# Outgoing transfers placed one iteration later on the transfer queue, and each state's row of C fetched by one transfer instead of two

## The chip, the cores and the metric

The kernel runs on one core of a Trainium2 chip. The metric is the device time of one execution in microseconds. A core has five engines that each work through their own list of instructions in order: TensorE (PE in the profile, with its weight loads as PEld), VectorE (DVE), ScalarE (ACT), GpSimd (POOL) and SyncE (SP). In this kernel every transfer between on-chip memory (SBUF) and device memory (HBM) is issued by SP. SP waits in order: a transfer whose data are not ready holds up every transfer behind it. The bytes are moved by 16 DMA engines of the core.

## The reference

The input is 8 images of 64 x 64 tokens with 96 channels. Layer 0 is a two-dimensional state-space block, layer 1 an attention without softmax followed by a quantized feed-forward layer. What matters here is the state-space part:

```python
xs = jnp.stack([s0, s1, s0[..., ::-1], s1[..., ::-1]], axis=1)       # 4 directions of 4096 tokens, 192 channels
x_dbl = jnp.einsum('bkdl,kcd->bkcl', xs, x_proj_weight)
dts, Bs, Cs = jnp.split(x_dbl, [DT_RANK, DT_RANK + D_STATE], axis=2) # 6, 16, 16 rows
delta = jax.nn.softplus(jnp.einsum('bkrl,kdr->bkdl', dts, dt_projs_weight) + dt_projs_bias[None, :, :, None])
def step(hst, inp):                                                 # h has 192 x 16 states for each image and direction
    u_t, d_t, B_t, C_t = inp
    hst = hst * jnp.exp(d_t[..., None] * A) + (d_t * u_t)[..., None] * B_t[:, :, None, :]
    return (hst, jnp.einsum('bkdn,bkn->bkd', hst, C_t))
```

Every one of the 16 states n has its own row C[n] over the tokens, and the state of every channel is multiplied by that same row.

## The kernel before

**The scan.** A step m is one image, one pair of directions (q = 0 forward, q = 1 backward) and one chunk of T = 512 tokens; there are 8 x 2 x 8 = 128 steps. The 128 partitions hold two directions of 64 channels each, and G = 3 groups make up the 192 channels. The main loop at the end of `run` has one iteration for each step and state: 128 x 16 = 2048 iterations. In iteration i, ScalarE makes the decays for state i + 2 (`decay`, L966) and on some states the products with B (`times_b`, L988), VectorE scans state i (`recur`, L1009), TensorE brings the products of state i + 1 into PSUM (`turn`, L996) and adds up state i - 4 (`reduce`, L1044), and GpSimd multiplies state i - 1 by its row of C (`read`, L1030).

**The rows of C.** `prologue` computes the projected rows of a step, writes the 32 rows of C (2 directions x 16 states) to a buffer `crow` in HBM (L910), and `fetch` reads them back, one state at a time, copied to 64 partitions for each direction (L957):

```python
cc = made[m].c[n] = pool.tile([P, T], F32, tag="cc", name=f"cc_{i}", bufs=5)
for d in range(2):
    nc.sync.dma_start(
        out=cc[d * GC : (d + 1) * GC], in_=made[m].crow[d * NS + n : d * NS + n + 1, :].to_broadcast([GC, T])
    )
```

`fetch(i + 4)` is the last thing of iteration i. There are five `cc` buffers, so it takes the buffer that `read(i - 1)` of the same iteration has just used, and SP waits for GpSimd there.

**The work beside the scan.** While one image is scanned, the next image's front (normalization, convolution, the walk along the diagonals: `front`) and the last image's tail (join of the four directions, attention, feed-forward: `tail`) run in the gaps. They are Python generators that a planner, the class `Work`, advances. A generator yields the engine that its next piece needs ("A", "V", "G", "P"), its estimated time and how many iterations it has to lie back; `LAGS` has the defaults, and `proceed` keeps the iteration from which the piece may be placed. `next` opens an iteration and places the pieces with the tag "S"; `at("A")`, `at("V")` and so on are called at fixed places of the iteration. `finish` runs iterations without the scan until a condition holds; it is called at the seventh iteration of every image, to see that the streams of work of the image before have ended.

**The outgoing transfers.** A generator issues a transfer out of SBUF directly behind the instruction that makes its data, in the same piece. So the transfer stands on SP's list ahead of the `fetch` of that iteration. These are the gate and the convolved image (`convolve`, L561 and L568), the walked sequence (`walk`, L599), the middle result and the transposed tokens (`join`, L689 and L728), the output (`layers`, L834), the rows of C (`prologue`, L910), and a step's sums (`place`, L1072, and `spread`, L1089). Some of what comes in matters as well: `join` loads its tiles `y` at L634 into buffers that L728 has read from two or three chunks before.

Of the kernel before, what the change touches and what calls it, by code (L numbers as in the profile page):

```python
# [254 lines left out]
    return "P", us, lag, "long" if long else "short"  # L255


SPIN = ("P", 0.0, -1, False)


class Work:
# [104 lines left out]
    def finish(self, enough):  # L366

        self.alone = True
        while not enough():
            self.next()  # L370
            for tag, place in (("A", 0), ("V", 0), ("P", 2), ("G", 0)):
                self.at(tag, place)
        self.alone = False
        self.credit = dict.fromkeys(self.PLACES, 0.0)

    def hurry(self, enough):

        self.alone = self.hurried = True
        while not enough():
            self.now += 1  # L380
            for tag, place in (("A", 0), ("V", 0), ("P", 2), ("G", 0)):
                self.at(tag, place)
        self.alone = self.hurried = False

# [89 lines left out]
def front(tc, work, x, k, at, b):  # L474
# [8 lines left out]
    with tc.tile_pool(name=f"f1_{b}", bufs=1, **area) as p1, tc.tile_pool(name=f"f2_{b}", bufs=2, **area) as p2:  # L483
        flat = p1.tile([DM + 1, WP * WP + 4], F32, tag="xp", name="xp")
        xp = flat[:, 0 : WP * WP].rearrange("p (h w) -> p h w", w=WP)

        def clear():
            yield gp(4.0)

            nc.gpsimd.memset(flat[0:DM, 0 : WP + 1], 0.0)  # L490
            nc.gpsimd.memset(flat[0:DM, WP * (WP - 1) - 1 :], 0.0)
            nc.gpsimd.memset(flat[0:DM, 2 * WP - 1 : 2 * WP - 1 + HH * WP].rearrange("p (h w) -> p h w", w=WP)[:, :, 0:2], 0.0)
            nc.gpsimd.memset(flat[DM : DM + 1], 1.0)
            while not at.measured:
                yield SPIN

        yield [clear()], 1

        normed = set()

        def norm(c):

            xt = fetched(nc, p2, x, b, c, 3)
            ps = yield bank(0.45, 4)
            v = channels(nc, k, ps, xt)
            yield act(0.65)
            nc.scalar.activation(
                xp[0:DM, 1 + 8 * c : 9 + 8 * c, 1 : WW + 1], v.rearrange("p (h w) -> p h w", w=WW),
                AF.Identity, scale=at.norm[:, 0:1], bias=at.norm[:, 1:2],
            )  # L510
            work.release(ps)
            normed.add(c)

        TILES = HH * WP // P
        groups = [range(4 * c, min(4 * c + 4, TILES) if c < NCH - 1 else TILES) for c in range(NCH)]

        def convolve(c):

            pre = p2.tile([P, 5, DI], F32, tag="pre", name="pre")
            z = p2.tile([HC, 2, CH], F32, tag="z", name="z")  # L520
            while not all(r in normed for r in range(min(c + 2, NCH))):
                yield SPIN
            left = [0]

            def out(ps, to, v):
                left[0] += 1
                yield dve(0.6, 1)
                nc.vector.tensor_copy(to, v)
                work.release(ps)
                left[0] -= 1  # L530

            tiles = groups[c]
            for first in range(0, len(tiles), 2):
                some = tiles[first : first + 2]
                ps = yield bank(0.33, 0, True)
                v = view(ps, P, len(some), DI)
                for j, t in enumerate(some):
                    for i in range(9):
                        if i or j:
                            yield pe(0.33)  # L540
                        o = t * P + i // 3 * WP + i % 3
                        nc.tensor.matmul(  # L542
                            v[:, j, :], flat[:, o : o + P], k.wf[:, i, :], start=(i == 0), stop=(i == 8), skip_group_check=True
                        )
                work.full(ps)
                work.start(out(ps, pre[:, first : first + len(some), :], v))
            for a in range(2):
                ps = yield bank(0.85, 0)
                nc.tensor.matmul(
                    view(ps, HC, CH // WW, WW), k.w_in[:, DI + a * HC : DI + (a + 1) * HC],  # L550
                    xp[0:DM, 1 + 8 * c : 9 + 8 * c, 1 : WW + 1], start=True, stop=True,
                )
                work.start(out(ps, z[:, a, :], view(ps, HC, CH)))
            yield pe(0.0, 1)
            while left[0]:
                yield SPIN
            yield act(4.5)
            nc.scalar.activation(pre[:, 0 : len(tiles), :], pre[:, 0 : len(tiles), :], AF.Silu)
            nc.scalar.activation(z, z, AF.Silu)
            k.tables()  # L560
            nc.sync.dma_start(out=at.gate[:, :, c * CH : (c + 1) * CH], in_=z)  # L561

            image = at.image[0 : HH * DOUBLE].rearrange("(h a x c) -> h x a c", a=2, c=DI, x=WW)
            for j, t in enumerate(tiles):
                for h in range(t * P // WP, min((t * P + P - 1) // WP + 1, HH)):
                    lo, hi = max(t * P, h * WP), min(t * P + P, h * WP + WW)
                    if lo < hi:
                        nc.sync.dma_start(  # L568
                            out=image[h, lo - h * WP : hi - h * WP],
                            in_=pre[lo - t * P : hi - t * P, j, :].unsqueeze(1).to_broadcast([hi - lo, 2, DI]),  # L570
                        )

        ahead = [norm(c) for c in range(3)]
        yield ahead + [j(c + 3 * (j is norm)) for c in range(NCH) for j in (convolve, norm) if j is convolve or c + 3 < NCH], 4

    with tc.tile_pool(name=f"f3_{b}", bufs=3, **area) as p2:

        def walk(c):
# [12 lines left out]
            for g in range(G):  # L591
                ps = yield bank(0.45, 4 if g == 0 else 0)
                for i in range(TB):
                    nc.tensor.transpose(ps[:, i * P : (i + 1) * P], ut[:, i, g].rearrange("p d i -> p (d i)"), k.ident)
                yield act(0.6)
                nc.scalar.copy(u[:, g, :], ps)
                work.release(ps)
            for d in range(2):
                nc.sync.dma_start(  # L599
                    out=at.seq[d][:, c * T : (c + 1) * T].rearrange("(g i) t -> i g t", i=GC),  # L600
                    in_=u[d * GC : (d + 1) * GC],
                )
# [5 lines left out]
def tail(tc, work, x, out, k, at, b, last=False):  # L608
# [4 lines left out]
    with tc.tile_pool(name=f"t1_{b}", bufs=1, **area) as p1:  # L613
# [5 lines left out]
        with tc.tile_pool(name=f"t2_{b}", bufs=8 if last else 2, **area) as p2:  # L619
# [3 lines left out]
            def join(c):  # L623
# [61 lines left out]
                        )  # L685
                yield act(0.5)
                nc.scalar.copy(t, po)
                if not last:
                    nc.sync.dma_start(out=at.mid[:, s, :], in_=t)  # L689
                work.release(ps)  # L690
                yield dve(1.7)
                for i in range(4):
# [32 lines left out]
                if last:  # L725
                    kept[c] = t, xaT
                else:
                    nc.sync.dma_start(out=at.turned[:, c * CH : (c + 1) * CH], in_=xaT)  # L728
                joined.add(c)

# [31 lines left out]
        with tc.tile_pool(name=f"t3_{b}", bufs=8 if last else 3, **area) as p2:  # L762

            def layers(c):
# [66 lines left out]
                yield gp(2.0)  # L831
                nc.gpsimd.tensor_tensor(y16, y16, k.b2q, ALU.add)
                nc.gpsimd.tensor_tensor(t, t, y16, ALU.add)
                nc.sync.dma_start(out=out[b].rearrange("(t p) c -> p t c", p=P)[:, s, :], in_=t)  # L834

            yield [layers(c) for c in range(NCH)], 8 if last else 3
# [2 lines left out]
def run(tc, psum, dram, x, out, w, NB):  # L839
# [39 lines left out]
    def prologue(m):  # L879
# [26 lines left out]
        x = o.x = tile("x", [NX, T])  # L906
        nc.scalar.activation(x, v, AF.Identity, bias=w.xb)  # L907
        work.release(ps)
        o.crow = dram.tile([2 * NS, T], F32, tag="crow", name=f"crow_{m}", bufs=3)
        nc.sync.dma_start(out=o.crow, in_=x[XC:NX, :])  # L910


        delta = tile("delta", [P, G, T])
        for g in range(G):
            ps = yield bank(0.85)
            nc.tensor.matmul(ps, w.ws[:, q, g, :], x[0 : 2 * NR + 1, :], start=True, stop=True)  # L916
            yield dve(0.6)
            nc.vector.tensor_copy(delta[:, g, :], ps)  # L918
            work.release(ps)
# [32 lines left out]
    def fetch(i):  # L952

        m, n = divmod(i, NS)
        cc = made[m].c[n] = pool.tile([P, T], F32, tag="cc", name=f"cc_{i}", bufs=5)
        for d in range(2):
            nc.sync.dma_start(  # L957
                out=cc[d * GC : (d + 1) * GC], in_=made[m].crow[d * NS + n : d * NS + n + 1, :].to_broadcast([GC, T])
            )

    def decay(i):
        m, n = divmod(i, NS)
# [95 lines left out]
    def place(m):  # L1058
# [7 lines left out]
        for d in range(2):  # L1066
# [1 line left out]
                rows[:, d].rearrange("p k (g i) -> p k g i", i=GC),  # L1068
                y.rearrange("p (k g) (d i) -> p d k g i", g=G, d=2)[:, d],
            )  # L1070
        if q == 0:
            nc.sync.dma_start(out=image(b).part[:, c, :], in_=ys)  # L1072
        else:
            work.start(spread(m, rows), urgent=True)

    def spread(m, rows):
        b, q, c = steps[m]
        for d in range(2):
            yield gp(1.8, 1)
            nc.gpsimd.tensor_tensor(  # L1080
                rows[:, d], rows[:, d], other[m].rearrange("p (d k c) -> p d k c", d=2, k=TB)[:, d], ALU.add
            )
            stride = (3 * WW + 1) * DI if d == 0 else (3 * WW - 1) * DI
            for v in range(2):
                for again in range(2):
# [194 lines left out]
```

## Time and profile before

| what | value |
|---|---|
| time, median of 3 runs | 11243.42 us (11231.5 to 11244.23) |
| the profiled execution's own time | 11245.66 us |
| its span, first to last instruction | 11243.9 us |
| PE, DVE, ACT, POOL busy | 81%, 84%, 84%, 83% of the span |
| PE weight loads busy | 68% of the span |
| L1030 on POOL (state times C) | 2048 x 3457 ns = 7079.9 us |
| L1009 on DVE (the scan) | 5376 x 1262 ns and 768 x 1201 ns |
| DMA packets | 1122742, 1206.98 MB, 107 GB/s on average |
| share of the 16 DMA engines' time | 40.3% |
| mean granted TensorE clock | 0.907 |

All four computing engines are busy for more than four fifths of the span, none of them all the time. The table's busy times are of one profiled execution. "Share of the DMA engines' time" is the time that all packets took, over 16 times the span. In the profile "SPq" is SP as the issuer of transfers, and a line such as "DMA cc<-crow" is a transfer between its issue and its landing.

### The profile page before, as it was taken

How to read it: one execution, taken by the hardware profiler on the slowest of the kernel's cores; microseconds unless marked ns; L12 is line 12 of the kernel's file. 1: busy time of each engine (PE TensorE's matmuls, PEld its weight loads, DVE VectorE, ACT ScalarE, POOL GpSimd, SP SyncE). 2: the span in 40 equal slices, each digit the busy share in tenths (PEclk: the TensorE clock that was granted, in tenths of full speed). 3: DMA queues.
4: the chain of work that ended last, by engine and by line, in shares of the span. 5: the costliest groups of instructions: out<-in, count | busy, mean ns of one | idle time of the engine just before them, and what ended most of it. 6: DMA issues, size and time to landing. Idle time of an engine off the chain costs nothing.

```text
span 11243.9 us, 182845 instructions
## 1 busy us (share of the span) xinstructions
PE 9140.0 (81%) x60885; PEld 7661.4 (68%) x60885; DVE 9396.9 (84%) x10582; ACT 9455.9 (84%) x19651; POOL 9365.4 (83%) x7047
## 2 busy tenths in 40 slices
PE   6888788878888788878888788887888878878884
PEld 5677677666676667766677666776667666666663
DVE  2988988888888888888888888888898888989993
ACT  3888888888888888888888888888898888888883
POOL 1877987899878998789987899779997799998994
PEclk8999999888998889988999898998999988889886
DMA  3335333543335443354334543345433543432332
GB/s 91 106 92 143 100 98 92 144 118 102 97 93 149 110 108 95 96 144 113 102 92 113 138 107 102 92 118 134 109 99 90 133 119 104 108 103 84 99 94 63
DMA packets 1122742, 1206.98 MB, mean 107 GB/s; under 512 B 452790, under 2 KB 730007, under 8 KB 1121799
## 3 DMA queue, kind: packets, MB, share of 16 engines
q1 hardware_dynamic: 1121798, 1195.28, 40.3%
q8 instruction: 485, 7.95, 0.3%
q14 instruction: 459, 3.75, 0.1%
HBM read 874.83 MB, written 319.98 MB: 106 GB/s over the span
## 4 chain that ended last, share of the span: by engine, by line
PE 24%; ACT 23%; DVE 17%; POOL 14%; issue 10%; DMA 7%; SPq 4%; DVEq 0%; POOLq 0%; ACTq 0%
DVE h L1009 11%; ACT feedT L988 9%; POOL h L1030 8%; ACT decay L966 7%; PE y L1044 7%; PE feed L996 7%; DMA cc<-crow 4%; DVE feed L1013 4%; PE bank L542 3%; SPq L587 2%; PE bank L894 2%; PE feed L998 1%; ACT L63 1%; POOL du L928 1%; DMA y<-wide 1%
## 5 line engine op out<-in xcount | busy, mean ns | idle before, releaser
L1030 POOL TENSOR_TENSOR h<-h,cc 128x1536 f32<-128x1536 f32 x2048 | 7079.9, 3457 | 458.3 <-DMA cc<-crow 228.9
L1009 DVE TENSOR_TENSOR_SCAN h<-decay,carry,feed 128x512 f32<-128x512 f32 x5376 | 6514.2, 1262 | 810.2 <-PE feed L996 704.8
L966 ACT ACTIVATE decay<-delta,a_neg 128x512 f32<-128x512 f32 x6144 | 3975.0, 714 | 1116.4 <-DVE h L1009 1114.4
L996 PE MATMUL feed<-ident,feedT 128*128 128x128 f32 x16896 | 3090.8, 303 | 1649.1 <-DVE h L1009 1084.6
L1044 PE MATMUL y<-ident,h 128*128 128x128 f32 x24576 | 3847.4, 290 | 130.7 <-POOL h L1030 47.4
L996 PEld LDWEIGHTS feed<-ident,feedT 128*128 128x128 f32 x16896 | 2209.1, 155 | 2246.9 <-ACT feedT L988 840.8
L988 ACT ACTIVATE feedT<-duT,rows 128x192 f32<-128x192 f32 x10240 | 3673.7, 445 | 17.6 <-PE feed L996 14.7
L1044 PEld LDWEIGHTS y<-ident,h 128*128 128x128 f32 x24576 | 3164.5, 152 | 525.2 <-issue 410.3
L1013 DVE TENSOR_TENSOR feed<-feed,du 128x512 f32<-128x512 f32 x1920 | 1200.4, 685 | 162.2 <-PE feed L998 146.5
L1025 POOL COPY carry<-h 128x3 f32<-128x3 f32 x2048 | 402.5, 197 | 877.0 <-DVE h L1009 803.2
L1009 DVE TENSOR_TENSOR_SCAN h<-decay,feed 128x512 f32<-128x512 f32 x768 | 879.5, 1201 | 118.9 <-PE feed L996 106.8
L542 PE MATMUL bank<-wf,xp 97*128 97x192 f32 x4266 | 851.9, 332 | 0.0
L998 PE MATMUL feed<-x,pick 77*128 77x512 f32 x1280 | 708.8, 636 | 3.9
L542 PEld LDWEIGHTS bank<-wf,xp 97*128 97x128 f32 x4266 | 692.8, 194 | 5.4 <-issue 4.6
L928 POOL TENSOR_TENSOR du<-delta,u 128x1536 f32<-128x1536 f32 x128 | 448.4, 3503 | 188.8 <-ACT delta L921 188.8
L916 PE MATMUL bank<-x,ws 13*128 13x512 f32 x764 | 435.5, 650 | 5.6 <-ACT x L907 5.6
L979 POOL TENSOR_TENSOR feedT<-duT,rows 128x512 f32<-128x512 f32 x384 | 396.2, 1060 | 4.7 <-PE feed L996 4.7
L894 PE MATMUL bank<-wx,u 128*128 128x77 f32 x3048 | 360.0, 275 | 0.0
L894 PEld LDWEIGHTS bank<-wx,u 128*128 128x128 f32 x3048 | 352.3, 193 | 1.9 <-ACT duT L936 0.2
L918 DVE COPY delta<-bank 128x512 f32<-128x512 f32 x382 | 256.7, 672 | 86.5 <-PE bank L916 86.1
L934 PE MATMUL bank<-ident,du 128*128 128x128 f32 x1532 | 251.8, 291 | 65.1 <-POOL du L928 61.8
L998 PEld LDWEIGHTS feed<-x,pick 77*128 77x128 f32 x1280 | 211.5, 200 | 97.6 <-DVE h L1009 44.8
(261 smaller groups left out, 6957.4 us busy)
## 6 DMA issues: line engine op xcount, KB each, us to landing
cc<-crow SPq DMA_DIRECT2D x4096, 128.0 KB
u<-seq SPq DMA_DIRECT2D x256, 384.0 KB
wide<-ys SPq DMA_DIRECT2D x512, 192.0 KB
ut<-image SPq DMA_DIRECT2D x768, 64.0 KB
seq<-us SPq DMA_DIRECT2D x128, 384.0 KB
part<-ys SPq DMA_DIRECT2D x64, 768.0 KB
y<-part SPq DMA_DIRECT2D x64, 768.0 KB
y<-wide SPq DMA_DIRECT2D x256, 192.0 KB
```

The costliest lines, as they stand in the source:

```text
L542: nc.tensor.matmul(v[:, j, :], flat[:, o : o + P], k.wf[:, i, :], start=(i == 0), stop=(i == 8), skip_group_check=True)
L894: nc.tensor.matmul(v[:, j, :], u[:, g, j * P : (j + 1) * P], w.wx[:, q, g, :], start=(g == 0), stop=(g == G - 1))
L916: nc.tensor.matmul(ps, w.ws[:, q, g, :], x[0 : 2 * NR + 1, :], start=True, stop=True)
L928: nc.gpsimd.tensor_tensor(du, delta, u, ALU.mult)
L966: nc.scalar.activation(decays[i][:, g, :], made[m].delta[:, g, :], AF.Exp, scale=w.a_neg[:, q, g, n : n + 1])
L988: nc.scalar.activation(f[part], o.duT[part], AF.Copy, scale=o.rows[:, j, XB + d * NS + n : XB + d * NS + n + 1])
L996: nc.tensor.transpose(feed[g][:, j * P : (j + 1) * P], feeds[i][:, j * G + g, :], w.ident)
L998: nc.tensor.matmul(feed[0], w.pick[:, FEED[:n].count("D"), :], made[m].x, start=True, stop=True)
L1009: nc.vector.tensor_tensor_scan(h[:, g, back], a[:, g, back], feed[g][:, back], init, ALU.mult, ALU.add)
L1013: nc.vector.tensor_tensor(feed[g], feed[0], made[m].du[:, g, :], ALU.mult)
L1030: nc.gpsimd.tensor_tensor(hs[i], hs[i], c.unsqueeze(1).to_broadcast([P, G, T]), ALU.mult)
L1044: nc.tensor.matmul(y[:, j, :], hs[i][:, g, r * P : (r + 1) * P], w.ident, is_transpose=True, start=(n == 0 and j % 4 == 0), stop=(n == NS ...
```

## The change

A transfer out of SBUF no longer follows its data in the same piece. Its generator first yields `LATER`, a piece of no time with the tag "S" that may be placed one iteration on, and issues the transfer when it is resumed by `next`, at the beginning of the following iteration and so behind the `fetch` of the iteration that made the data. The transfer of the middle result moves from L689 to the end of the join, beside L728. `place` hands its transfer to a small generator of its own, `first_rows`. `finish` and `hurry` place "S" pieces too. The first of the three `delta` products in `prologue` is allowed to follow without further lag. In `fetch` the two transfers, one for each direction, become one, whose source is a view of `crow` with the directions outermost, then a repetition of 64, then the row.

```diff
+LATER = ("S", 0.0, 1, False)
 SPIN = ("P", 0.0, -1, False)
...
     def finish(self, enough):
-            for tag, place in (("A", 0), ("V", 0), ("P", 2), ("G", 0)):
+            for tag, place in (("A", 0), ("V", 0), ("P", 2), ("G", 0), ("S", 0)):
...
     def hurry(self, enough):
-            for tag, place in (("A", 0), ("V", 0), ("P", 2), ("G", 0)):
+            for tag, place in (("S", 0), ("A", 0), ("V", 0), ("P", 2), ("G", 0)):
...
             nc.scalar.activation(z, z, AF.Silu)
             k.tables()
+            yield LATER
             nc.sync.dma_start(out=at.gate[:, :, c * CH : (c + 1) * CH], in_=z)
...
                 work.release(ps)
+            yield LATER
             for d in range(2):
                 nc.sync.dma_start(
                     out=at.seq[d][:, c * T : (c + 1) * T].rearrange("(g i) t -> i g t", i=GC),
...
                 nc.scalar.copy(t, po)
-                if not last:
-                    nc.sync.dma_start(out=at.mid[:, s, :], in_=t)
                 work.release(ps)
...
                 else:
+                    yield LATER
+                    nc.sync.dma_start(out=at.mid[:, s, :], in_=t)
                     nc.sync.dma_start(out=at.turned[:, c * CH : (c + 1) * CH], in_=xaT)
                 joined.add(c)
...
                 nc.gpsimd.tensor_tensor(t, t, y16, ALU.add)
+                yield LATER
                 nc.sync.dma_start(out=out[b].rearrange("(t p) c -> p t c", p=P)[:, s, :], in_=t)
...
         work.release(ps)
+        yield LATER
         o.crow = dram.tile([2 * NS, T], F32, tag="crow", name=f"crow_{m}", bufs=3)
         nc.sync.dma_start(out=o.crow, in_=x[XC:NX, :])
         delta = tile("delta", [P, G, T])
         for g in range(G):
-            ps = yield bank(0.85)
+            ps = yield bank(0.85, None if g else 0)
...
         cc = made[m].c[n] = pool.tile([P, T], F32, tag="cc", name=f"cc_{i}", bufs=5)
-        for d in range(2):
-            nc.sync.dma_start(
-                out=cc[d * GC : (d + 1) * GC], in_=made[m].crow[d * NS + n : d * NS + n + 1, :].to_broadcast([GC, T])
-            )
+        nc.sync.dma_start(
+            out=cc, in_=made[m].crow.rearrange("(d n) t -> d n t", n=NS)[:, n : n + 1, :].to_broadcast([2, GC, T])
+        )
...
-        if q == 0:
-            nc.sync.dma_start(out=image(b).part[:, c, :], in_=ys)
-        else:
-            work.start(spread(m, rows), urgent=True)
+        work.start(spread(m, rows) if q else first_rows(m, ys), urgent=True)
+
+    def first_rows(m, ys):
+        b, _, c = steps[m]
+        yield LATER
+        nc.sync.dma_start(out=image(b).part[:, c, :], in_=ys)
...
     def spread(m, rows):
         for d in range(2):
             yield gp(1.8, 1)
             nc.gpsimd.tensor_tensor(
                 rows[:, d], rows[:, d], other[m].rearrange("p (d k c) -> p d k c", d=2, k=TB)[:, d], ALU.add
             )
+            yield LATER
```

## The prediction

> **What bounds the kernel now.** I read the page first, then SP's waits, the tile `cc`, the chain, and windows over the transfers that stand out. The page's chain and DMA parts:
>
> ```profile
> PE 24%; ACT 23%; DVE 17%; POOL 14%; issue 10%; DMA 7%; SPq 4%; DVEq 0%; POOLq 0%; ACTq 0%
> ...
> q1 hardware_dynamic: 1121798, 1195.28, 40.3%
> ...
> cc<-crow SPq DMA_DIRECT2D x4096, 128.0 KB
> ```
>
> No engine carries the end: the chain goes round four of them, and DMA with SP have 11% of it. The 16 DMA engines are 40% busy as a mean. The second line holds packets, MB and share. What SP waits for (total us, times, longest):
>
> ```profile
> SPq L957 <- POOL carry L1025: 1982.1, 682, 8.8
> SPq L957 <- POOL h L1030: 1410.5, 484, 7.2
> SPq L1072 <- ACT ys L1067: 399.2, 49, 12.1
> SPq L561 <- ACT z L559: 352.6, 64, 7.3
> ...
> SPq L634 <- DMA turned<-y: 177.9, 35, 7.1
> ```
>
> The first two are `fetch` waiting for its buffer, once an iteration; this is slack. Lines 3 and 4 are what the change goes at: a transfer placed too early, with `fetch` behind it. From the answer on the tile `cc`, its issues (shortest, median and longest in ns, first and last start in us) and what POOL lost to it:
>
> ```profile
> L957 SPq DMA_DIRECT2D cc<-crow x4096: 444/588/2621, 224.4 to 10984.2; - x196
> ...
>   DMA cc<-crow: 228.9, 34
> ```
>
> So 2048 iterations take 10,759.8 us, 5.25 us each, and late rows of C stop POOL for 228.9 us in all. Now two pieces of the chain, and the window in which the second is nearly alone (us, busy of five engines, clock, DMA share, GB/s):
>
> ```profile
> 1840.32 5.92 DMA image<-pre
> ```
>
> ```profile
> 5000.42 10.22 DMA turned<-y
> 5010.66 0.57 SPq L634
> ```
>
> ```profile
> 5007.00:5010.00 3.00, 3.00 (x24) 2.47 (x23) 2.52 (x4) 3.00 (x7) 3.00 (x2) 1.00 0.07 26
> ```
>
> These carry my forecast. `turned<-y` is 97 rows of 2 KB and lands after 10.22 us; the `cc` transfers, 64 such rows, land after a median of 3.26 us by the trace's semaphore records. In the window the DMA share is 0.07, one engine of sixteen (0.0625), and 26 GB/s is all that moves: the packet records show one 2 KB packet after another, 84 ns each. The whole transfer runs on one engine. The `image<-pre` at 1840.32 has 62 rows of 2 x 768 B and takes 5.92 us, where those of 64 rows land after a median of 2.71 us; its semaphore shows two counts at 5.57 and 5.92 us and all others at once at 0.62 us, so two engines carried it. The records of the others read the same way: 10 rows, 10 late counts; 14 rows, 14; 22 rows, 11; 64 rows, 16. In this trace, a transfer is spread over as many engines, up to 16, as divide its outermost count.
>
> **The change, part by part.** The median of the runs is 11243.42 us; the profiled run took 11245.66 with a span of 11243.9, so 1.8 us lie outside the span. I sum on the profiled run.
>
> *One transfer for a row of C.* It removes 2048 of SP's 4096 issues at L957. At the median of 588 ns this is 1,204 us of SP time, and it hides in `fetch`'s 3,390 us of waits for POOL. The new source has 2 as its outermost count (directions), then a repetition of 64, then 512 elements; the destination has 128 rows. The trace has no transfer whose two sides differ like this, so it could go to 2 engines or to 16. A share of work for each engine has to be a whole share of both sides; the rows with counts of 62 and 58 (two engines both) are the nearest, and I take 2. The bytes stay the same, 262,144 an iteration, but before, each engine had 8 rows of 2 KB; now each of two has 64. At 84 ns a row this is 5.38 us an iteration, above today's 5.25 before any other traffic: over the kernel, 131,072 rows x 84 ns = 11,010 us on each of the two. From below, 26 GB/s makes 78.8 ns a row and 10,330 us; from above I allow 88 ns and 11,534.
>
> The same two engines have the rest to carry. All packets took 40.3% x 16 x 11,243.9 = 72,500 engine-us; the 262,144 of `cc` at 84 ns are 22,020 of that, at the mean of all 2 KB packets (118.5 ns) 31,060. What remains is 2,590 to 3,155 us for each engine. The first engine also has all 112 transfers of 97 rows (L728, L774): 112 x 97 x 84 ns = 913 us, 856 above its mean share, and some 150 us of narrow `image` transfers (estimated from their row counts at 36 to 48 ns a packet of 768 B). That gives 3,600 to 4,160. With every kind at its undisturbed packet time it is 2,950. Fourteen engines lose `cc`, so packets should meet less; I take 3,300.
>
> The first 224 us and the 260 after the last issue hold no `cc`; the first engine's part in them, some 150 us, is in the sum already, which leaves 333 us. Together: 11,010 + 3,300 + 333 = 14,643 us, if the first engine never idles between.
>
> It will idle a little. `y<-wide` (L634) waits for `turned<-y`, which now queues behind up to four `cc` transfers on the same engine; SP then stands with `fetch` behind it, the queue runs dry, and it takes some 4 us from the last packet to the next `cc` packet (the 10.22 us above less 97 x 84 ns leave 2.07, issues of 0.6 us each the rest): 56 x 4 = 224 us. With the 1.8 us outside the span: 14,643 + 224 + 2 = 14,869.
>
> One sentence each on two rules of the Trainium skill, "DMA: Bandwidth & Descriptors", that pull apart here. Its section "Rules for kernel authors" advises one 128-partition transfer over two to disjoint partition halves; by that the sum would be that of my first rival. Its section "Why a DMA increments its semaphore by 16 and not by 1" says that the engines are the largest number up to 16 that divides the slowest counts of both sides, which is 2 for this source, as in my forecast. The trace agrees with the second as far as it goes (62 rows, two late counts); no run so far shows the first.
>
> *Transfers an iteration later.* They move past one `fetch` on SP's list. SP's waits at L561, L1072, L1089 and L910 (352.6 + 399.2 + 514.7 + 230.6 us, the last two added up from the same view) should nearly vanish, since their data are then an iteration old. That is worth at most the 228.9 us of POOL above plus parts of the chain's 8.2% in `cc` transfers (4.2%) and SP (4%), 922 us. Those parts overlap, and the next late thing (PE waiting for DVE 1,084.6 us, ACT for DVE 1,114.4) stands close behind; I put it at 300 us if SP is what is late, and at nothing where the DMA engines are the bound.
>
> *What is lost by it.* `spread` yields twice more and `layers` once more, so at the seventh iteration of an image they are not done, and `finish` runs rounds without the scan: by the planner's own counting, none before, now 1 for the first image and 3 for each of the six after, 19 in all. Their price lies between nothing (engines still work off what was placed) and a full iteration each, 19 x 5.25 = 100 us. Behind up to four queued `cc` transfers (21.5 us) they are hidden, so I take nothing. The later `crow` and the moved `delta` product have a whole step, 16 iterations, before they are needed: nothing.
>
> **The rivals.** *First, on the other side: the row is spread over 16 engines.* If the share goes by the destination's 128 rows, the bytes and the spread are as before, SP is freer and the 300 us come: 11,244 - 300 = 10,944. For it speaks that the trace has no transfer with two such sides and that the destination has 128 rows; against it that a leading count has ruled wherever the trace shows one. The number of engines decides: with k of them `cc` costs 22,020 / k us on each, and with the 3,300 beside it this must stay under 10,760. At 3 it is 10,640, the turning point; at 4 it is 8,805 and hidden.
>
> *Second: it is spread, but SP was never what was late.* Then the extra rounds are all there is: up to 11,244 + 100 = 11,344.
>
> *Third: confined to two engines, and slower for each row.* Today's mean 2 KB packet takes 118.5 ns, with 16 engines at once. If that comes from all reading the same row in HBM and not from their number, 131,072 x 118.5 ns = 15,530, plus 4,160 and 333: 20,023. Against it: the median of `cc` packets in quiet stretches is also 84 ns.
>
> **How the numbers follow.** The forecast, two engines at about 84 ns, has 0.85; the first rival 0.09, the second 0.02, the third 0.04. The forecast's own ends: low 10,330 + 2,950 + 333 = 13,613; high 11,534 + 4,160 + 333 and an idle 5 us behind each of the 112 one-engine transfers, 560, make 16,587. So 13,600 to 16,600, which holds most of the 0.85 and leaves the rivals out. A measurement here can tell about 0.2% (22 us) from no change. Faster by more: 0.09, within: 0.01, slower by more: 0.90.
>
> **What would show it.** L957 issues 2048 transfers, DMA share of the page near 30%, GB/s near 81 for the same bytes. `POOL h <- DMA cc<-crow` grows from 228.9 us to some 3,000 or more and leads the waits; DMA has most of the chain; busy shares fall to some 63%. In calm stretches the DMA share is near 2 of 16 (0.13 to 0.2) at about 50 GB/s. The forecast is wrong if `cc` lands within 4 us in calm stretches and POOL hardly waits for it. The lag is right if the waits at L561 and L1072 drop below some 50 us each, and without value if the time would be the same with them.

## The result

The changed kernel takes 14,628.82 us (median of 4 runs, 14,622.09 to 14,632.22) against 11,243.83 us beside it: 1.3011 times as long, 95% interval 1.2989 to 1.3034. That is slower by 30%, 241 us below the predicted 14,870. The profiled execution has a span of 14,619.9 us.

The page of the changed kernel, beside the parts that were shown of the kernel before (engines' busy us and share; the queue's packets, MB and share of 16 engines; the chain's shares; the transfers of `cc`):

```profile
PE 9889.2 (68%) x60885; PEld 8353.5 (57%) x60885; DVE 9446.4 (65%) x10582; ACT 9507.8 (65%) x19651; POOL 9306.7 (64%) x7047
...
q1 hardware_dynamic: 1060358, 1195.04, 27.7%
...
DMA 47%; POOL 16%; PE 14%; SPq 9%; ACT 6%; DVE 5%; issue 4%; POOLq 0%; DVEq 0%; ACTq 0%
...
cc<-crow SPq DMA_DIRECT2D x2048, 256.0 KB
```

VectorE, ScalarE and GpSimd have nearly the work that they had (9,446, 9,508 and 9,307 us, from 9,397, 9,456 and 9,365) and 30% more time to do it in. The same bytes move, the sixteen DMA engines are less busy as a mean than before (27.7% for 40.3%), and yet the chain is now a DMA chain: 47% of it. A mean over sixteen engines hides two that are full. A calm stretch shows them (us, busy of five engines, clock, DMA share, GB/s):

```profile
5024.00:5040.00 16.00, 9.41 (x82) 8.73 (x80) 6.25 (x6) 14.92 (x35) 7.78 (x7) 1.00 0.13 50
```

0.13 is two engines of sixteen (0.125), and 50 GB/s is twice what `turned<-y` had alone on one. This is no chosen stretch alone: by the packet records, exactly two packets are under way in 8,734 of the 14,126 us between the first and the last issue of a row of C. From the chain in that stretch, one row of C and the multiplication that waited for it, and from the answer on the tile `cc`, its issues (L961 now, L957 before) and what GpSimd lost to it:

```profile
5019.55 15.67 DMA cc<-crow
5035.29 0.10 issue
5035.39 3.43 POOL h L1034
```

```profile
L961 SPq DMA_DIRECT2D cc<-crow x2048: 487/3344/8483, 224.0 to 14350.2; - x187
...
  DMA cc<-crow: 4074.0, 1252
```

An iteration takes (14,350.2 - 224.0) / 2,048 = 6.90 us, from 5.25. The multiplication, L1030 before and L1034 now, waited 228.9 us for rows of C in 34 iterations; now it waits 4,074 us in 1,252. By the trace's semaphore records a row lands a median of 17.6 us after the start of its issue (5th to 95th percentile 10.0 to 21.3), where it was 3.26. Each of the 2,048 transfers leaves three records on its semaphore, one with its issue and two late ones. Each of the 4,096 before left sixteen.

### The profile page after: what moved, and what is told of

The parts are those of the page before. It is cut to its first block, busy times and chain, and to the rows that moved or that the text cites. A ratio compares the mean times of both kernels' runs of the same rounds, so it can differ in the third digit from the quotient of the medians.

```text
span 14619.9 us, 179050 instructions
## 1 busy us (share of the span) xinstructions
PE 9889.2 (68%) x60885; PEld 8353.5 (57%) x60885; DVE 9446.4 (65%) x10582; ACT 9507.8 (65%) x19651; POOL 9306.7 (64%) x7047
## 3 DMA queue, kind: packets, MB, share of 16 engines
q1 hardware_dynamic: 1060358, 1195.04, 27.7%
## 4 chain that ended last, share of the span: by engine, by line
DMA 47%; POOL 16%; PE 14%; SPq 9%; ACT 6%; DVE 5%; issue 4%; POOLq 0%; DVEq 0%; ACTq 0%
DMA cc<-crow 39%; POOL h L1034 9%; PE feed L1000 3%; PE y L1048 3%; DVE h L1013 3%; DMA gate<-z 3%; ACT feedT L992 2%; ACT decay L970 2%; POOL du L933 2%; PE bank L543 2%; SPq L961 2%; SPq L1096 2%; DMA u<-seq 1%; DVE feed L1017 1%; PE bank L898 1%
## 5 line engine op out<-in xcount | busy, mean ns | idle before, releaser
L1034 POOL TENSOR_TENSOR h<-h,cc 128x1536 f32<-128x1536 f32 x2048 | 7068.0, 3451 | 4793.9 <-DMA cc<-crow 4074.0
L1000 PE MATMUL feed<-ident,feedT 128*128 128x128 f32 x16896 | 3189.5, 318 | 1919.4 <-DVE h L1013 1168.1
L1048 PE MATMUL y<-ident,h 128*128 128x128 f32 x24576 | 4112.8, 304 | 179.7 <-POOL h L1034 169.3
L1048 PEld LDWEIGHTS y<-ident,h 128*128 128x128 f32 x24576 | 3419.4, 161 | 622.2 <-issue 388.2
L1000 PEld LDWEIGHTS feed<-ident,feedT 128*128 128x128 f32 x16896 | 2396.2, 166 | 2411.8 <-DVE h L1013 663.2
L941 ACT COPY duT<-bank 128x512 f32<-128x512 f32 x383 | 220.7, 576 | 903.2 <-PE bank L939 902.7
L939 PEld LDWEIGHTS bank<-ident,du 128*128 128x128 f32 x1532 | 204.4, 161 | 827.6 <-POOL du L933 827.0
L898 PE MATMUL bank<-wx,u 128*128 128x77 f32 x3048 | 426.9, 305 | 204.5 <-DMA u<-seq 199.0
L898 PEld LDWEIGHTS bank<-wx,u 128*128 128x128 f32 x3048 | 413.4, 220 | 219.1 <-issue 181.1
L598 ACT COPY us<-bank 128x512 f32<-128x512 f32 x187 | 107.7, 578 | 540.8 <-PE bank L596 477.7
L596 PE MATMUL bank<-ident,ut 128*128 128x128 f32 x748 | 148.4, 335 | 415.4 <-DMA ut<-image 415.0
```

The source lines that it names most:

```text
L898: nc.tensor.matmul(v[:, j, :], u[:, g, j * P : (j + 1) * P], w.wx[:, q, g, :], start=(g == 0), stop=(g == G - 1))
L1000: nc.tensor.transpose(feed[g][:, j * P : (j + 1) * P], feeds[i][:, j * G + g, :], w.ident)
L1034: nc.gpsimd.tensor_tensor(hs[i], hs[i], c.unsqueeze(1).to_broadcast([P, G, T]), ALU.mult)
L1048: nc.tensor.matmul(y[:, j, :], hs[i][:, g, r * P : (r + 1) * P], w.ident, is_transpose=True, start=(n == 0 and j % 4 == 0), stop=(n == NS ...
```

## The experiments

The theory is that a row of C now runs on two DMA engines, as its source's outermost count is 2, and that these two are full. The rivals: the later placing, or the rounds without the scan, cost the time; one large transfer is slow in itself; the row only comes late.

**The two parts of the change, each alone.** The first run puts the old `fetch` back into the changed kernel:

```diff
-        nc.sync.dma_start(
-            out=cc, in_=made[m].crow.rearrange("(d n) t -> d n t", n=NS)[:, n : n + 1, :].to_broadcast([2, GC, T])
-        )
+        for d in range(2):
+            nc.sync.dma_start(
+                out=cc[d * GC : (d + 1) * GC], in_=made[m].crow[d * NS + n : d * NS + n + 1, :].to_broadcast([GC, T])
+            )
```

> The change with the two transfers for each row of C put back; the outgoing transfers stay an iteration later. Theory (the whole loss is the row of C on two DMA engines): the loss is gone, 10,950 to 11,250 us; the prediction's 300 us of gain from a freer SP would make 10,944, and the waits at L563 and L1080 are below 50 us each. Rival (the later placing and its 19 rounds without the scan cost time themselves): 11,300 us or more, up to 14,600 if they are the whole cause.

The second makes the opposite edit to the kernel before.

> The kernel before with the one transfer for a row of C alone; the outgoing transfers stay where they were. Theory (two engines carry every row): 14,500 to 14,900 us, within 2% of the changed kernel, and POOL waits some 4,000 us for the row of C. Rival (the late placing is needed to make the loss, for example because transfers now queue behind the row): below 13,000 us.

Later placing alone: 11,234.66 us, 0.9989 of the kernel before (0.998 to 0.9998). One transfer alone: 14,643.41 us, 1.3024 (1.3006 to 1.3041), which is the whole loss. The late row of C is there as well, in GpSimd's waits of the second run:

```profile
POOL h L1029 <- DMA cc<-crow: 4011.6, 1180, 28.1
```

The first run's expectation was only half met: SP's waits at the two lines that it names did fall, from 352.6 and 399.2 us to 115.2 and 101.7 and not below 50, and the time hardly followed. SP's waits in that run, and what GpSimd lost to `cc`:

```profile
SPq L563 <- ACT z L560: 115.2, 53, 8.1
SPq L1081 <- ACT ys L1072: 101.7, 37, 9.0
...
SPq L915 <- ACT x L911: 61.0, 29, 12.2
```

```profile
  DMA cc<-crow: 129.3, 34
```

**More engines for the same transfer.** These two keep one transfer for a row of C and give its source another outermost count, by writing each row several times to HBM; here for a count of 4:

```diff
-        o.crow = dram.tile([2 * NS, T], F32, tag="crow", name=f"crow_{m}", bufs=3)
-        nc.sync.dma_start(out=o.crow, in_=x[XC:NX, :])
+        o.crow = dram.tile([NS, 2, 2, T], F32, tag="crow", name=f"crow_{m}", bufs=3)
+        for d in range(2):
+            nc.sync.dma_start(
+                out=o.crow[:, d], in_=x[XC + d * NS : XC + (d + 1) * NS, :].unsqueeze(1).to_broadcast([NS, 2, T])
+            )
...
-            out=cc, in_=made[m].crow.rearrange("(d n) t -> d n t", n=NS)[:, n : n + 1, :].to_broadcast([2, GC, T])
+            out=cc,
+            in_=made[m].crow.rearrange("n d r t -> n (d r) t")[n].unsqueeze(1).to_broadcast([4, 32, T]),
```

> The changed kernel, with each row of C written twice to HBM, so that the one transfer that reads it has an outermost count of 4 instead of 2. Theory (a transfer is spread over as many engines as divide both sides' outermost counts): the row costs 32 x 84 ns = 2.7 us of each of four engines an iteration, 5,505 us in all; with about 2,900 us of other traffic this is under the 10,760 us of the scan, so the time falls back to 10,950 to 11,450 us; in calm stretches the share of the DMA engines shows four at once. Rival (one large transfer is slow in itself, or its source being read 64 times is): 14,000 us or more.

For 16, the two counts of 2 in the row's buffer become 2 and 8, and the transfer repeats each of 16 rows 8 times.

> The changed kernel, with each row of C written eight times to HBM, so that the one transfer has an outermost count of 16. The traffic grows by 512 KB minus 64 KB a step. Theory: 16 engines, 8 rows each, as the two transfers had; 10,900 to 11,300 us, and if SP's 2048 saved issues are worth anything, below the run that only places transfers later. Rival (SP was never late): the same as that run within 0.3%, or slower by the extra writes.

Four engines: 11,403.11 us, 1.0143 (1.0129 to 1.0157). Sixteen: 11,229.74 us, 0.9984 (0.9974 to 0.9994). The semaphores have five records for each transfer in the first (one at once, four late) and sixteen in the second. From the answer on `cc` with sixteen engines:

```profile
L964 SPq DMA_DIRECT2D cc<-crow x2048: 514/520/2597, 228.0 to 10933.0; - x187
...
  DMA cc<-crow: 102.2, 13
```

In a calm stretch with four engines:

```profile
3412.00:3416.00 4.00, 3.90 (x25) 2.50 (x24) 4.00 (x5) 3.84 (x7) 1.96 (x1) 1.00 0.26 102
```

0.26 and twice the bytes of two engines. So the count rules, not the size of the transfer. Reading one row in HBM many times is not it either: the kernel before reads each row 64 times too, and its transfers land after a median of 3.26 us. The run with four also shows that "hidden" by the sum over the kernel is not hidden everywhere: rows land after a median of 6.38 us, but 13.3 at the 95th percentile, and GpSimd waits for them

```profile
  DMA cc<-crow: 302.7, 60
```

which is 173 us more than in the run that only places transfers later; that run is 168 us faster.

**Bytes or pieces.** GpSimd reads half a row twice over, and the transfer brings only that half; the other half of each row of C is left out of the computation:

```diff
-            out=cc, in_=made[m].crow.rearrange("(d n) t -> d n t", n=NS)[:, n : n + 1, :].to_broadcast([2, GC, T])
+            out=cc[:, 0 : T // 2],
+            in_=made[m].crow.rearrange("(d n) t -> d n t", n=NS)[:, n : n + 1, 0 : T // 2].to_broadcast([2, GC, T // 2]),
...
-        nc.gpsimd.tensor_tensor(hs[i], hs[i], c.unsqueeze(1).to_broadcast([P, G, T]), ALU.mult)
+        h = hs[i].rearrange("p g (a t) -> p (g a) t", a=2)
+        nc.gpsimd.tensor_tensor(h, h, c[:, 0 : T // 2].unsqueeze(1).to_broadcast([P, 2 * G, T // 2]), ALU.mult)
```

> The changed kernel, with the one transfer cut to the first half of each row of C (1 KB instead of 2 KB; still 128 pieces, outermost count 2); GpSimd uses that half for both halves of the tokens, so the second half of the row is left out of the computation. Theory (the time of two engines, by bytes): a piece should take about 44 ns, the row 64 x 44 = 2.8 us an iteration, so the engines have room again and the time falls to 11,200 to 11,700 us. Rival (the number of pieces, or SP's issue of 3.3 us, is what costs): 13,500 us or more.

A single execution took 11,449.78 us, against 11,246.99 beside it. The 1 KB packets took a median of 46 ns. From the answer on `cc` (issues in ns: shortest, median, longest; GpSimd's waits):

```profile
L961 SPq DMA_DIRECT2D cc<-crow x2048: 482/507/5963, 224.3 to 11184.5; - x187
...
  DMA cc<-crow: 363.5, 60
```

Still two engines (three semaphore records each), still 128 pieces, and nearly all of the loss is gone; the wait for `cc` is down from 4,074 us to 363.5. SP's issue is back at a median of 507 ns from 3,344, so the long issue was a consequence of the full engines and not a cause.

**Throughput or lateness.** Six buffers in place of five, and `fetch(i + 5)` for `fetch(i + 4)`.

> The changed kernel with six buffers for the rows of C and a fetch five iterations ahead instead of four. Theory (two engines are full, no row can come sooner): 14,500 to 14,750 us, as the changed kernel. Rival (a row comes too late because its way is long, and an earlier issue would hide it): one more row under way of five, some 10 to 20% less, 12,000 to 13,200 us.

A single execution took 14,638.32 us, the changed kernel's time.

```profile
L961 SPq DMA_DIRECT2D cc<-crow x2048: 487/3354/8642, 223.4 to 14362.5; - x187
...
  DMA cc<-crow: 3782.1, 1224
```

The issues end at the same time, and the wait for `cc` is nearly as long. An earlier issue brings nothing where the engines are full.

**Where the later placing's gain went.** Added to the first run, so that the next image's work starts when the last one's has ended and no round without the scan is run for it:

```diff
             if at == LAG + 3 and b:
-                work.finish(lambda: all_done() and not other)
-                work.finish(all_done)
+                late = True
+            if late and all_done() and not other:
+                late = False
                 work.stream(between(b))
```

> The run that only places transfers later, with the 19 rounds without the scan taken out: the next streams start when the old ones have ended, and nothing is placed alone for that. Theory A (the rounds take back what the later placing gains): 40 to 100 us below the run with the rounds, 11,130 to 11,200 us. Theory B (the rounds are hidden, and SP was hardly ever late; VectorE's and TensorE's waits take the place): within 25 us of it, 11,210 to 11,260 us.

11,164.37 us, 0.993 (0.9917 to 0.9942). Against the first run's 0.9989 that is 0.0059 x 11,244 = 66 us (by the two intervals some 17 more or less), 3.5 us for each of the 19 rounds. Theory A holds: the later placing without the rounds is worth some 79 us, and with them 12. The traces show only a part of the 66 us at the rounds themselves: the multiplication behind them starts 10.8 to 11.8 us after the one before it in the six images with three rounds, where it is 5.4 us without rounds; in the image with one round it is 5.4 us in both runs. That adds up to 36 us. The edit also moves the start of the next image's work, and where the other 30 us lie is not shown.

**Other narrow transfers, and a version faster than both kernels.** The 97 rows of L728 and L774, on one engine each time, are split:

```diff
-                    nc.sync.dma_start(out=at.turned[:, c * CH : (c + 1) * CH], in_=xaT)
+                    for lo, hi in ((0, DM), (DM, DM + 1)):
+                        nc.sync.dma_start(out=at.turned[lo:hi, c * CH : (c + 1) * CH], in_=xaT[lo:hi])
...
-                    nc.sync.dma_start(out=xaT, in_=at.turned[:, c * CH : (c + 1) * CH])
+                    for lo, hi in ((0, DM), (DM, DM + 1)):
+                        nc.sync.dma_start(out=xaT[lo:hi], in_=at.turned[lo:hi, c * CH : (c + 1) * CH])
```

First on the kernel before, alone:

> The kernel before with nothing but the transfers of 97 rows (L728, L774) split into 96 rows and one row. Theory (97 rows on one engine hold SP up at L634, 177.9 us, and what comes in behind): SP's wait for turned<-y nearly vanishes; 11,170 to 11,230 us. Rival (that wait was slack): within 15 us of 11,244 us.

11,222.13 us against 11,258.21 beside it, 0.997 (0.9958 to 0.9982): as the theory had it. SP's wait for `turned<-y`, 177.9 us before, is no longer among its waits. Then with everything together:

> A candidate for the best: the later placing, the one transfer on 16 engines, no rounds without the scan, and the transfers of 97 rows split into 96 rows and one, so that 16 engines carry the 96. Theory: SP's wait for turned<-y (161.8 us) and the late y<-wide behind it go; with the run on 16 engines at 11,230 us, 11,100 to 11,220 us. Rival (the next late thing stands close behind everywhere): within 25 us of 11,230 us.

11,137.38 us, 0.9902 (0.9887 to 0.9917): some 1% faster than the kernel before. Last, what the one transfer on 16 engines has in it:

> The candidate for the best with the two transfers for a row of C put back; it tells what the one transfer on 16 engines is worth. Theory (SP is no longer late, so its 2048 issues are worth nothing): within 15 us of 11,137 us. Rival (SP's time counts): 11,150 to 11,170 us, near the run without rounds.

11,166.43 us, 0.9924 (0.9911 to 0.9936), so 29 us above, but in another set of runs, with a slower kernel before beside it. Both were repeated side by side:

> The candidate for the best once more, beside the next run on the same chip. Theory (2048 issues fewer let SP place the next transfers earlier): some 20 to 30 us below the next run. Rival (SP's issues are worth nothing, the difference was one of chips): within 10 us of it.

> The same with two transfers for a row of C, beside the run above. Theory: ratio to the kernel before of about 0.992, the run above 0.990. Rival: both the same within 0.001.

0.9899 (0.9886 to 0.9912) for the one transfer, 0.9915 (0.9899 to 0.993) for two, 11,130.02 and 11,147.28 us. The two are 17 us apart, between the first expectation's theory (20 to 30) and its rival (within 10); the ratios are those of the second's theory (0.990 and 0.992). But the intervals overlap: whether SP's 2,048 saved issues are worth some 17 us or nothing stays open. The same holds for the split on top of the other edits, 0.9924 and 0.9915 where it was 0.993 without it.

## Why the prediction was right

**Two engines.** The step that carried the forecast is shown. The count of 2 against 128 destination rows, which no transfer of the trace before had, gives two engines, as the narrow transfers of one count on both sides had suggested. The page "DMA: Bandwidth & Descriptors" of the Trainium skill says so for unequal counts ("Why a DMA increments its semaphore by 16 and not by 1"), and this case's runs with 2, 4 and 16 agree. Its advice for one 128-partition transfer over two halves ("Rules for kernel authors") cost 30% here at a source count of 2 and 1.4% at 4; at 16 the one transfer took what the two took, within the intervals (0.9984 and 0.9989).

**The size.** 131,072 rows at the measured median of 85 ns (of all 2 KB packets, 70% of them rows of C) are 11,141 us on each of the two engines, where the prediction had 11,010. The 14,126 us between the first and last issue then leave 2,985 us for everything else on the first engine, idle time included. The prediction had 3,300 for the rest, less 150 at the ends, and 224 us idle: 3,374. So what was too large is the rest and the idle time together; the lower end of the rest, 2,950 with every packet undisturbed, lay nearer. How the 2,985 us divide is not shown, since the packet records do not name the engine: no packet of this queue is under way in 66.8 us of that stretch, which is only the least that the first engine can have been idle. The two errors, 131 us too little and 389 too much, partly cancel, and to that extent the closeness is luck. (224 and 260 less 150 are 334, not 333; this is 1 us.) The mechanism given for the idle time is not what happened: SP hardly stands at L637, L634 before, for the 97 rows,

```profile
SPq L637 <- DMA turned<-y: 45.0, 35, 2.8
```

where it waited 177.9 us before. That its own long issues now keep it back is likely, but no run tests it.

**Later placing.** Here the prediction was wrong where it did not decide. It put 300 us on it, from GpSimd's 228.9 us and a part of the chain's 8.2%; the runs show 79 without the rounds. GpSimd's wait for `cc` fell only from 228.9 to 129.3 us, and some of the late arrivals have another cause: splitting the 97 rows alone, in the kernel before, brings it to 193.4. Of the waits that the prediction had close behind, PE's for DVE did not change (1,085.5 us, from 1,084.6) and ACT's for DVE fell only from 1,114.4 to 991.8. The share of a chain was no measure of a gain. The 19 rounds were counted right, and with the two transfers for a row of C they cost up to 3.5 us each, two thirds of the upper end of 5.25, of which the traces show 1.9 at the rounds. In the changed kernel the later placing is hidden, as was taken: 1.3011 with it and 1.3024 without it, with overlapping intervals.

**The rivals.** The first, sixteen engines, is what the run with 16 shows, but at 11,230 us, not at 10,944. Its turning point was right as a sum, not as a promise: at four engines 1.4% remains. The third, slower rows, is excluded by the 85 ns and by a time 5,400 us below its sum.

## What to carry to other kernels

Before two transfers are merged, look at the outermost count of both sides of the new one: here 2 made two engines of sixteen carry 537 of 1,206 MB, four still cost 1.4%, and sixteen cost nothing that these runs can tell. A low mean share of the DMA engines says nothing of the fullest one; a calm window whose share is a small multiple of 1/16, and the number of late semaphore counts, told here how many engines a transfer had. If work is put off in a schedule that is checked for its end at a fixed place, look at what waits there: the wait can cost what the putting off gained.

## What the runs showed of the hardware that was not expected

SP's own issue of a transfer becomes long when the engines behind it are full: the median for `cc` rose from 588 to 3,344 ns, 8,483 at most, and 6,724 us of SP's time in all against 2,509 for twice as many issues. Where the engines had room it was 507 to 529 ns for the same one transfer.

The granted TensorE clock was lower in the slower kernel, 0.808 against 0.907 over the span, and its mean L1044 matmul took 304 ns (now L1048) against 290, with TensorE at 68% against 81% of the span. No run here separates the cause.
